# Four image blocks on one core: an involution's start, its passage to a convolution, and a Fourier gate's end, re-staged

## The chip, the cores and the metric

The kernel runs on one core of a Trainium2 chip, as one program with one launch. Its time is the device time in microseconds; three runs of the kernel before give 1874.28, 1877.03 and 1877.57 us, median 1877.03. Lower is better. The profile comes from one further execution of 1874.37 us, whose recorded span is 1872.6 us.

## The reference

The input is x, 4 images of 256 channels and 56 x 56 pixels, in float32. Four residual layers follow each other, each on the group norm of its input (32 groups of 8 channels, `_gn`):

```python
x = x + L0(_gn(x))   # involution: 7x7 taps computed per pixel, one tap set per 16 channels
x = x + L1(_gn(x))   # two 3x3 convolutions, 256 to 256 channels, with batch norms and ReLU
x = x + L2(_gn(x))   # involution again, with batch norms and ReLU
x = x + L3(_gn(x))   # Fourier gates:
    cf = sigmoid((real part of fft2(x), mean over pixels) @ W.T + b)     # one per channel
    sf = real part of fft2(mean of x over the channels)                  # one per pixel
    out = x * cf + x * sf
```

The mean of a two-dimensional transform over all its frequencies is the pixel at the origin, so cf needs only the first pixel of each channel (`first_of`). sf needs the channel mean and two small products with cosine and sine matrices.

An involution multiplies the normed input by a 64-row weight (`red`), giving 64 numbers per pixel, and these by `span`, giving 16 x 49 taps per pixel. Each tap multiplies the pixel at its offset, and the 49 results are added.

## The kernel before

**Blocks and units.** An image is two blocks of 128 channels (`cb` 0 and 1); a block is a tile of 128 x 3136 (1.6 MB) from a pool of three buffers (`new_block`). Eight units (image, block) run through the first involution, twelve row chunks through the convolutions, eight units through the second involution, and the gates of layer 3 run inside the second involution, an image behind. The results between the layers lie in DRAM (`src`).

**A unit of an involution** has two stages. In the first, `tap_matrices` (L471 to L489), 32 steps each make six products of the 64-row image `hp` (which lies in both halves of the partitions) with a table `z_sb`, three from each half. The result is copied out of PSUM with the bias table `zb_sb` added, by VectorE (L489) in three steps of four and by ScalarE (L482) in the fourth. In the second stage, `apply` (L513 to L540), seven columns of 8 pixels each multiply the taps `kt` by the windows `xw`. A column's windows are made three columns ahead: `next_strip` (L362, L364) norms a strip, `next_windows` transposes it (L381), copies it (L382) and shuffles it with four DMAs of `xw` into itself (L388, L390), 0.76 MB in all, issued by SP and in layer 0 partly by GpSimd.

**Work between.** Steps of other work are generators that are advanced at numbered steps of the first stage (`hooks`, steps 0 to 31) or after columns of the second (`late`): the sums of the next image (`sums`), the group norm (`norm_steps`: aggregate, product with `gavg_sb`, three VectorE steps, product, power on GpSimd, shift), the next image's 64 rows (`bottleneck`, L404 to L441), its loads. After `since = mark()`, `in_order(since)` binds each engine to the order in which the program was written; instructions before it are placed by a scheduler.

**Start of layer 0.** Both blocks of image 0 are loaded on SP in four pieces each. The norms of both are made, then `bottleneck(0)`: weights scaled by the norm (`redn`, L404), products for 9 image rows at a time in two halves of 64 output rows (L433), copied on ScalarE (L450) and across the halves by VectorE (L441). `make_tables` loads `span` on ScalarE's queue, copies it into `z_sb` (16 copies on VectorE, L300; two of biases, L308), makes the bias table by 24 products (L315) and copies it (L322). `batch_norms` follows. The same tables for layer 2 are made in unit 0, at steps 3, 14 and 21, and stored to DRAM on SP (L747, L748); the load of image 1 stands at step 23.

**Passage to the convolutions.** After the first column of unit 7, `begin_conv` issues on SP the first rows (L889) and both halves of the raw weights (L897, 1.18 MB each); the shuffles of the columns behind it stand after these on SP. The norm of the last block (L197 to L212) runs after the last column. The convolution begins with `row_weights` (loads L952, L953 on ScalarE's queue; six steps L964 to L966 on VectorE), `phases` (four on ScalarE, L1039, four on VectorE, L1037), `transform` (L1047 to L1069), and the first products (L1160).

**End of layer 3.** For the last image nothing else runs beside. After the norm, `channel_mean` scales a column of ones by the norm (L585), multiplies it with the block, 448 pixels at a time (L593, L596), adds the shift (L604), and turns the row of means into 56 x 56 by a store to DRAM and a load back (L607, L608). `gate_factors` loads the weights of cf (L616), makes cf (L623, L630), the first Fourier product (L639) and its copy `half` (L649). `last_gates` computes, for each of seven chunks of 8 image rows, the second Fourier product as eight products of 56 columns, each with one row of `half` spread over 128 columns as its weights (L700). Then per block: norm (L710), (sf + cf) times it (L713), add to the block (L715, block 0 on GpSimd, block 1 on VectorE), store (L716, GpSimd's and SP's queues).

## Time and profile before

| what | us |
|---|---|
| median of three runs | 1877.03 |
| profiled execution | 1874.37 |
| its span | 1872.6 |
| TensorE products busy | 1709.5 (91%) |
| weight loads busy | 1509.6 (81%) |
| VectorE busy | 1433.3 (77%) |
| ScalarE busy | 748.8 (40%) |
| GpSimd busy | 432.2 (23%) |
| first column product (L513) of unit 0 | starts at 74.02 |
| first convolution product (L1160) | starts at 548.45 |
| last GpSimd store (L716) | issued from 1864.57 |

A float32 product appears as two records in the trace, so "x48" of L315 is 24 products; a transpose is one. PE is the product, PEld its weight load. In the chain of waits each row has a start, a length and what ran or was waited for, followed back from the last instruction. In a table of windows the columns are the window, its length, the busy time of PE, PEld, VectorE, ScalarE and GpSimd with the number of instructions, the clock granted to TensorE as a share of full speed, the share of the 16 DMA engines and their rate.

### The profile page before, as it was taken

To read this page: it belongs to the slowest core of one execution; us is meant where nothing else is said; L and a number is where in the kernel's file an instruction comes from. 1 tells how busy PE (TensorE), PEld (TensorE's weight loads), DVE (VectorE), ACT (ScalarE), POOL (GpSimd) and SP (SyncE) were. 2 spreads that over 40 slices of the span, in tenths; PEclk is the share of its full clock that TensorE was granted. 3 is DMA by queue.
4 is the path that set the end of the run, shared out by engine and by line. 5 is a ranking of instruction groups with operands and counts; after the bars stand their busy time and mean duration, and the time that the engine had idled before them with its cause. 6 is when DMAs were issued, how large, how long until landed. Compare 5 with 4: busy or idle time off the path is not lost.

```text
span 1872.6 us, 55573 instructions
## 1 busy us (share of the span) xinstructions
PE 1709.5 (91%) x24030; PEld 1509.6 (81%) x24030; DVE 1433.3 (77%) x2823; ACT 748.8 (40%) x1657; POOL 432.2 (23%) x615
## 2 busy tenths in 40 slices
PE   5999999999759999999999999997999898898866
PEld 3888888888748988898899889885877777778865
DVE  5687777876678988898888988865767777777763
ACT  2445445454423222232223212114666565565532
POOL 2323433244210000000000000000000581681672
PEclk9999999999979999999999999998999999999995
DMA  3445544453533111110111210223533764773652
GB/s 97 150 146 177 153 120 140 152 153 111 160 121 100 42 60 61 61 67 36 62 58 57 73 35 33 89 76 89 174 107 132 231 193 147 222 215 105 177 147 76
DMA packets 65589, 215.72 MB, mean 115 GB/s; under 512 B 13564, under 2 KB 20528, under 8 KB 61504
## 3 DMA queue, kind: packets, MB, share of 16 engines
q1 hardware_dynamic: 44448, 141.62, 24.1%
q0 software_dynamic: 14848, 65.85, 10.9%
q10 hardware_dynamic: 6048, 4.68, 0.8%
q8 instruction: 190, 3.11, 0.7%
q14 instruction: 55, 0.45, 0.1%
HBM read 76.24 MB, written 49.16 MB: 67 GB/s over the span
## 4 chain that ended last, share of the span: by engine, by line
PE 65%; DVE 21%; DMA 5%; POOL 3%; issue 3%; ACT 2%; SPq 1%; POOLq 0%; ACTq 0%; DVEq 0%
PE mm L1242 20%; PE ps L513 14%; DVE kt L489 12%; PE mm L1160 10%; PE ps L471 7%; PE mm L1131 6%; PE ps L381 4%; DMA xw<-xw 3%; PE ps L433 2%; DVE un L533 2%; PE ps L700 1%; ACT hp L452 1%; PE ps L596 1%; DVE st L844 1%; DMA xs<-in_x_dram 1%
## 5 line engine op out<-in xcount | busy, mean ns | idle before, releaser
L513 PE MATMUL ps<-kt,xw 126*32 126x48 f32 (+1 forms) x12544 | 383.5, 236 | 56.9 <-DMA xw<-xw 21.3
L513 PEld LDWEIGHTS ps<-kt,xw 126*32 126x32 f32 (+1 forms) x12544 | 344.2, 122 | 102.4 <-issue 48.1
L471 PE MATMUL ps<-hp,z_sb 64*126 64x133 f32 x6144 | 389.0, 282 | 19.2 <-DVE kt L489 7.0
L471 PEld LDWEIGHTS ps<-hp,z_sb 64*126 64x126 f32 x6144 | 370.7, 189 | 34.1 <-DVE kt L489 8.7
L489 DVE TENSOR_TENSOR kt<-ps,zb_sb 126x798 f32<-126x798 f32 x384 | 357.9, 978 | 43.6 <-PE ps L471 43.1
L1242 PE MATMUL mm<-v,u_sb 128*128 128x280 f32 (+1 forms) x1728 | 384.9, 384 | 3.3 <-DVE v L1067 3.3
L1242 PEld LDWEIGHTS mm<-v,u_sb 128*128 128x128 f32 x1728 | 327.6, 190 | 57.8 <-DVE v L1067 3.6
L482 ACT ACTIVATE kt<-ps,zb_sb 126x133 f32<-126x133 f32 x768 | 224.0, 441 | 179.4 <-PE ps L471 179.4
L1160 PE MATMUL mm<-v,u_sb 128*128 128x252 f32 (+1 forms) x936 | 211.2, 386 | 12.6 <-DVE v L1051 12.6
L1160 PEld LDWEIGHTS mm<-v,u_sb 128*128 128x128 f32 x936 | 177.2, 190 | 42.9 <-issue 12.6
L533 DVE SCALAR_TENSOR_TENSOR un<-ps,par_sb,un 128x240 f32<-128x240 f32 x224 | 98.4, 457 | 103.1 <-ACT un L526 98.8
L533 DVE SCALAR_TENSOR_TENSOR un<-ps,s,un 128x240 f32<-128x240 f32 x224 | 102.3, 457 | 92.9 <-ACT un L528 88.7
L1279 POOL DMA_DIRECT2D x<-xs x24 | 13.1, 546 | 684.9 <-DVE xs L1278 539.5
L1227 ACT ACTIVATE res<-xs,shift,norm_sb 128x1120 f32<-128x1120 f32 (+1 forms) x24 | 30.2, 1260 | 235.2 <-DVE xs L1278 119.7
L538 POOL TENSOR_TENSOR xs<-un,xs 128x240 f32<-128x240 f32 x112 | 72.4, 665 | 224.2 <-DVE un L533 224.1
L382 ACT COPY xw<-ps 126x896 f32<-126x896 f32 x112 | 101.5, 907 | 49.6 <-PE ps L381 39.2
L381 PE MATMUL ps<-ident_sb,strip_sb 128*126 128x128 f32 x784 | 111.4, 282 | 1.6 <-DVE kt L489 0.8
L526 ACT ACTIVATE un<-ps,par_sb 128x240 f32<-128x240 f32 x112 | 50.1, 448 | 138.6 <-PE ps L513 136.7
L1131 PE MATMUL mm<-xs,u_sb 128*128 128x126 f32 (+1 forms) x792 | 98.3, 277 | 1.3 <-DVE xs L1094 1.0
L528 ACT ACTIVATE un<-ps,bn_t,s 128x240 f32<-128x240 f32 x112 | 60.1, 538 | 97.8 <-PE ps L513 93.7
L139 POOL TENSOR_TENSOR norm_sb<-norm_sb,mhalf 128x1 f32<-128x1 f32 x32 | 19.2, 602 | 341.7 <-DVE norm_sb L138 341.7
L1131 PEld LDWEIGHTS mm<-xs,u_sb 128*128 128x128 f32 x792 | 94.3, 191 | 2.7 <-issue 1.4
(194 smaller groups left out, 1973.0 us busy)
## 6 DMA issues: line engine op xcount, KB each, us to landing
xw<-xw SPq DMA_DIRECT2D x168, 252.0 KB
xw<-xw SPq DMA_DIRECT2D x224, 126.0 KB
xw<-xw POOLq DMA_DIRECT2D x56, 252.0 KB, 4.7
xs<-x SPq DMA_DIRECT2D x24, 560.0 KB
x<-xs POOLq DMA_DIRECT2D x8, 1568.0 KB, 7.9
xs<-x SPq DMA_DIRECT2D x8, 1568.0 KB
xs<-in_x_dram SPq DMA_DIRECT2D x6, 1568.0 KB
x<-xs SPq DMA_DIRECT2D x6, 1568.0 KB
```

The costliest lines, as they stand in the source:

```text
L381: nc.tensor.transpose(ps[:Q, k * P : (k + 1) * P], flat[:, k * Q : (k + 1) * Q], ident_sb)
L382: nc.scalar.copy(xw[:, :NSB, :], ps[:Q, : NSB * P].rearrange("q (n c) -> q n c", n=NSB))
L471: nc.tensor.matmul(ps[:Q, i, k * NT : (k + 1) * NT], z_sb[i * R : (i + 1) * R, cb * GB // 2 + gp, z0 : z0 + Q], hp[i * R : (i + 1) * R, py ...
L482: nc.scalar.activation(kt[:, g0 + i, pb, :, k], ps[:Q, i, k * NT : (k + 1) * NT], AF.Identity, bias=zb_sb[:, cb * GB + g0 + i, p0 + k : p0 ...
L489: nc.vector.tensor_tensor(kt[:, g0 : g0 + 2, pb], ps[:Q, :, : PB * NT].rearrange("q i (k t) -> q i t k", k=PB), zb_sb[:, cb * GB + g0 : cb ...
L513: nc.tensor.matmul(v[m * j : m * j + m, i, :, k * TP : (k + 1) * TP], xw[:, window(ty), m * j : m * j + m], kt[:, ng * j : ng * j + ng, :, ...
L528: nc.scalar.activation(part, o[0], AF.Identity, bias=bn["t4"][:, cb : cb + 1], scale=bn["s4"][ng][:, 0, cb : cb + 1])
L533: nc.vector.scalar_tensor_tensor(part, o[e], s, part, ALU.mult, ALU.add)
L538: nc.gpsimd.tensor_tensor(dst, u, dst, ALU.add)
L1131: nc.tensor.matmul(ps[:, co * m : (co + 1) * m], u[ci][:, co * P : (co + 1) * P], v2[:, e, : n // 2, ci * WT : (ci + 1) * WT], start=(ci = ...
L1160: nc.tensor.matmul(ps, u1_sb[:, ci, dy, k, co * P : (co + 1) * P], v[:, k, dy * NB + ci : (dy + n - 1) * NB + ci + 1 : NB, :], start=(j == 0),
L1242: nc.tensor.matmul(ps, u2_sb[:, ci, dy, k, co * P : (co + 1) * P], v[:, k, dy * NB + ci : (dy + n - 1) * NB + ci + 1 : NB, :], start=(j == 0),
```

## The change

- **Start (`begin`, `warm`, `load_block`).** Block 0 is loaded in two pieces, block 1 in four. `span`, biases and `red` are loaded on GpSimd's queue. ScalarE does a first small copy at once, and the 16 + 2 + 1 table copies. The products of block 0 with all 128 output rows (both halves alike) stand in TensorE's order before block 1's norm, in seven banks, and block 1's are added to them afterwards; the copies alternate between ScalarE and VectorE, without copies across the halves. TensorE gets 8, 2 and 8 products that nobody reads. All of this lies inside the written order. `batch_norms` is a generator, spread over the start and unit 0.
- **Unit 0.** The layer 2 tables are no longer made there; image 1's load moves from step 23 to step 16.
- **Last image of layer 0.** The layer 2 tables are made there: loads at step 16 of unit 6, the copies three at a time after its columns on ScalarE, the bias table in six pieces (after a column of unit 6 and at steps 3, 6, 10, 14 and 18 of unit 7), the stores at step 22.
- **Passage.** Rows and the second half of the raw weights are loaded at step 28 of unit 7 on SP, the first half in three parts after columns 0, 1 and 2 on ScalarE's queue. `row_weights` loads its two slices on SP. All eight `phases` of chunk 0 run on ScalarE. 28 products that nobody reads stand before the first of the convolution. The last block's norm is made inside the first convolution steps.
- **End.** Block 0's normed values are made ahead (`last_normed`); block 1's mean is made by group sums of the raw block: 56 products, one an image column, each with 56 weights columns and 16 moving ones, scaled by the norm afterwards and added on VectorE (`last_mean`). cf's weights are loaded at step 20 of the last unit. The second Fourier product is one 56 x 56 product, spread on VectorE into 8 rows a partition (`rows`, masked by `last_xn[0]`), and seven products of 448 columns. Block 1 is finished on ScalarE.

```diff
@@ start
-            for cb in range(NB):
-                if (0, cb) not in xs_of:
-                    load(0, cb, 3)
+            since = mark()
+            if layer == 0:
+                load(0, 0, (4, 3))
+                load(0, 1, (2, 2, 2, 1))
+
+                nc.scalar.copy(norm_sb[:, 3, B - 1, 1, :], mhalf)
...
-            def make_tables(z_sb, zb_sb, span, sb, scratch, eng):
+            def make_tables(z_sb, zb_sb, span, sb, scratch, eng, parts):
...
-                            nc.vector.tensor_copy(
+                            nc.scalar.copy(
                                 field(z_sb[half, cb * m + gp, :]),
                                 taps[half, cb, :, 2 * gp + i].rearrange("p (y x) -> p y x", x=KK),
                             )
+                            yield
...
+            def begin():
...
+                steps(tables, 17)
+                warm(8, xs_of[0, 0][:, :P])
+                steps(sums0, NCHUNK)
+                norm = norm_of(0, 0, 0, sums_of[0, 0])
+                steps(norm, 2)
+                next(folds)
+                steps(norm, 1)
+                warm(2, ident_sb)
+                steps(norm, 1)
+                steps(folds, 2)
+                steps(norm, 1)
+                steps(sums1, 2)
+                steps(norm, 1)
+                nc.vector.tensor_scalar_mul(redn[:, 0], red_sb[:, 0], rstd[:, 0:1])
+                steps(sums1, NCHUNK - 2)
+                next(tables)
+                warm(8, ident_sb)
...
+                for j in range(NH):
+                    products(j, 0)
+                steps(norm, 2)
...
+                for j in range(NH):
+                    products(j, 1)
...
@@ last image of layer 0
+                if last_image and cb == 0:
+                    g2 = tables2()
+                    place(hooks, g2, (16,))
+                elif last_image:
+                    place(hooks, g2, (3, 6, 10, 14, 18, 22, 23))
+                    hooks.setdefault(28, []).append(ahead[0])
...
+                if last_image and cb == 0:
+                    for tx in range(6):
+                        late[tx] += [step(g2)] * 3
+                elif last_image:
+                    for tx in range(3):
+                        late[tx].append(ahead[1 + tx])
...
@@ end
+            def last_mean(b, bank):
...
+                for x in range(W):
+                    nc.tensor.matmul(means[:, x // m, x % m, :], xs[:, x, :], by, start=True, stop=True)
+                yield
...
+                nc.vector.tensor_tensor(
+                    parts,
+                    means,
+                    scales[:, :ng].unsqueeze(1).unsqueeze(1).to_broadcast([H, 2, m, ng]),
+                    ALU.mult,
+                )
...
-                    for r in range(CR):
-                        y = j * CR + r
-                        nc.tensor.matmul(
-                            sf[:, r * W : (r + 1) * W],
-                            half[:, y : y + 1].to_broadcast([P, P]),
-                            cs2_sb,
-                            start=True,
-                            stop=True,
-                        )
+                    nc.tensor.matmul(sf, last_xn[1][:H, j : j + 1].to_broadcast([H, P]), rows, start=True, stop=True)
                     for cb in range(NB):
...
+                        if cb == 0:
+                            nc.gpsimd.tensor_tensor(xs, xs, xn, ALU.add)
+                            nc.gpsimd.dma_start(ov[b, cb][:, at], xs)
+                        else:
+                            nc.scalar.activation(xs, xn, AF.Identity, bias=back)
+                            nc.sync.dma_start(ov[b, cb][:, at], xs)
...
-            run(norm_of(layer + 1, b, cb, st))
...
@@ passage
     def begin_conv():
-        room["h"] = new_h()
-        room["rows"] = new_block()
         room["v2"] = new_block()
         load_rows(0, src[1])
-        for ci, t in enumerate((room["h"], room["v2"])):
-            nc.sync.dma_start(
-                t[:, : 9 * C], wc1[ci * P : (ci + 1) * P].rearrange("c k n -> c (k n)")
-            )
+        raw_weights(1, 0, 1, nc.sync)
+
+    def begin_weights(part):
+        if part == 0:
+            room["h"] = new_h()
+        raw_weights(0, part, 3, nc.scalar)
...
-                    nc.scalar.dma_start(u[:, ci, :, 0, :], w[:, :, 0, :])
-                    nc.scalar.dma_start(u[:, ci, :, 5, :], w[:, :, 2, :])
+                    nc.sync.dma_start(u[:, ci, :, 0, :], w[:, :, 0, :])
+                    nc.sync.dma_start(u[:, ci, :, 5, :], w[:, :, 2, :])
...
-            g = phases(0, nc.vector)
-            for _ in range(4):
-                next(g)
+            ps = one_bank()
+            for _ in range(28):
+                nc.tensor.matmul(ps[:, :P], ident_sb, ident_sb, start=True, stop=True)
             for _ in range(NB):
                 next(weights1)
-            run(g)
+            run(phases(0))
...
-            tail1, tail2, slow = [], [], []
+            tail1, tail2, slow = [], [], [norm_steps(st, one_bank, 1, B - 1, NB - 1)]
```

## The prediction

> **What bounds the kernel now.** I read the page first (TensorE busy 91% of the span, by far the busiest), then the chain of waits in order of time, then the stretches in which TensorE idles, as 4 us windows. The repeated units are bound by TensorE or VectorE and the change leaves their body alone; what it touches is three seams: the start, the passage from the first involution to the convolutions, and the end.
>
> The start, in the chain (start us, length us, what):
>
> ```profile
> 23.73 7.20 PE ps L433 x26
> 30.93 3.03 PE ps L315 x48
> 36.57 4.01 PE ps L471 x36
> 41.49 3.62 PE ps L471 x60
> ...
> 53.08 1.26 DVE xs L300 x8
> ...
> 57.17 3.95 PE ps L471 x36
> 61.12 2.74 PE ps L315 x48
> 63.86 8.10 PE ps L471 x108
> ...
> 74.02 3.22 PE ps L513 x97
> ```
>
> The first tap matrices begin at 36.57, after products (L433) and bias tables (L315). 36 of their records take 4.01 us there, 60 take 3.62 us at 41.49: the first run at half clock. At 53.08 VectorE copies the tables of the *second* involution, and at 61.12 TensorE makes them; the records around run at half clock again. So unit 0's tap stage lasts 37.5 us; that of unit 7 lasts 489.34 - 463.98 = 25.4.
>
> The passage:
>
> ```profile
> 497.56 3.25 PE ps L513 x103
> ...
> 502.57 16.40 DMA xw<-xw
> ...
> 519.11 10.28 PE ps L513 x251
> ...
> 543.05 2.81 DVE ph L1037 x4
> ...
> 548.45 30.35 PE mm L1160 x120
> ```
>
> The window shuffle (xw<-xw) of the fifth column, 0.76 MB a column, waits in the DMA rings behind 3.5 MB of convolution loads issued after the first column (L889, L897). The DMA share in that time is 0.86 to 1.06. Then 18.0 us pass between the last product (530.44) and the first of the convolution.
>
> The end, and its clock (columns of the second fence: window, length, busy PE, PEld, DVE, ACT, POOL, granted clock, DMA):
>
> ```profile
> 1826.31 3.05 PE ps L596 x14
> 1829.39 1.16 ACT xs L604 x2
> ...
> 1830.67 1.79 DMA m<-xs
> ...
> 1832.89 2.15 DMA xs<-in_w_dram
> ...
> 1838.16 20.71 PE ps L700 x96
> ```
>
> ```profile
> 1838.00:1842.00 4.00, 3.84 (x18) 3.87 (x19) 0.12 (x2) 1.35 (x3) 0.00 (x0) 0.50 0.00 0
> ```
>
> 24.1 us go to 56 products of 56 columns, at half clock; the weight loads are as busy as the products.
>
> **What the skill says.** "TensorE: Matmul & The Clock Gate", Part 1: the array runs at half clock until a window of about 3.4 us was busy, and falls back after an idle one. The trace agrees: in 1 us windows the clock changes at 33.4, 40.0, 57.1, 60.6, 64.0 and 67.4, all near multiples of 3.41 us apart. It adds something: the tables (16 columns a product) count as idle, since the window that holds them ends at half clock (64.0), and the 56-column products never warm it. The same page, "LDWEIGHTS": its time goes with the columns, not the rows. Here a 128-column load costs 24.0/112 = 0.214 us cold, twice the page's 128/1.2 GHz[...]. "DMA: Bandwidth & Descriptors", "Issuing engines are not separate DMA queues": all queues share 16 engines. The stall at 502.57 shows it, so a move between queues alone frees no bandwidth.
>
> **Start and unit 0.** I rebuild the time line. Same bytes as before, so block 0 is in at about 9.6 (before 9.36). VectorE sums its last three chunks to 11.4 (3 x 0.6), aggregate 0.34; TensorE 0.6; small steps 0.8; two warm products 0.85 (2 x 128 columns at half clock); TensorE 0.6: 14.0. The table copies on ScalarE (18, at an estimated 0.22 each from the 0.26 of one-column activations, L630) end before that. In TensorE's order now follow 48 table records, cold: 126-column loads in two row halves, 0.105 us each (the pace at 36.57, 4.01/36, is 0.11): 5.0, to 19.0. Eight warm products, cold, 0.43 each (two passes of 0.214): 22.4. The clock then rises. Block 0's seven products are 3136 columns of full width; L1242 shows 33.96 us for 72 products of 280 columns (144 records in the chain), 1.69 ns a column at full clock, so 5.3, and 0.3 for what runs cold: 28.0. (The old ones, two halves of 64 output rows side by side, take 0.42 us a product warm.) Here is the price of the new order: block 1's group sums (ready at 19.3, five chunks after the weight scaling at 16.1) are queued behind these. From 28.0: two products, small VectorE steps, the power on GpSimd (0.56), shift, weights: 3.1. Second products 5.3, last copies 0.7: first tap product at 37.1, warm. Removed from that path: six half copies (0.43 each) and their waits. Bounds: 33 if the tables run warm, 40 if block 0's products run cold.
>
> Unit 0's tap stage: 25.4 as unit 7, plus three window transposes (0.91 each): 28.1. First column product at 65.2, before 74.0: **gain 8.8**. The moved load of image 1 (step 16 instead of 23) stands behind nine shuffles whose sources are done by then: nothing.
>
> **Last image, tables of the second involution.** 48 table records warm are 2.8 us (2.74 at 61.12), cut in six. The 16 copies go to ScalarE, 40% busy, so free in unit 6's columns; their loads on SP wait for a store that lands 7.9 us after its issue at the unit's start, and stand half a tap stage later. In unit 7's tap stage TensorE had 384 records x 0.0603 = 23.2 us plus 0.76 for the norm, and VectorE 24 x 0.98 plus sums, so most of the 2.8 shows: **loss 2.5** (0.5 to 5 if PSUM rotation stutters).
>
> **Unit 7's columns.** Before 530.4 - 489.3 = 41.1 us. Without the stall: four columns at 4.13 (505.74 - 489.34 = 16.40) and three without transposes at 3.25: 26.2. What is late next: rows and half the weights (2.4 MB) are now issued at tap step 28, when the DMA share was 0.00 to 0.01 (475 to 493), about 8 us at 300 GB/s (279 and 334 GB/s in the windows from 4 to 12 us), so done near the first shuffle. The other half goes in three parts of 0.39 MB on ScalarE's queue beside three shuffles of 0.76 MB: 1.15 MB per 4.13 us is 278 GB/s, just under what the stall's windows moved. I allow 1.5 us. **Gain 13.4** (0 to 15).
>
> **Passage.** After the last product: copies, sums, GpSimd's adds 3.0 as before; scales 0.3; six weight steps at 0.96: 5.8; zeroing 0.2; three transform steps 2.4; 0.2: 11.9 against 18.0. Beside it ScalarE's eight phases (0.84 each, 6.7); before, ScalarE could not start until it had issued four loads (533.98 to 538.68), which SP now issues. They may end 1 us after VectorE is ready. The norm is off the path; its two products go into the convolution. **Gain 5** (2 to 6). The 28 warm products (0.21 each, 6 us) end about 5 us before the convolution starts, so they save the cold start (4 us at half clock, 2 us lost) only about half the time: **gain 1**.
>
> **End.** Last product before at 1818.4. Block 0's seven activations (0.69 each) follow on ScalarE, beside the rest. TensorE runs 56 mean products, 112 records with 56-column loads: 47 ns warm or 93 cold by the column rule, 5.2 to 10.4; strided loads appear nowhere in the trace, so I take 5.9 (mostly warm) and keep 12 as the far end; no reason allows less than 5. So 1824.3. Norm 3.0 (1822.17 to 1825.27 before); then VectorE: first, scales 0.5, 896-element multiply out of PSUM 1.0 (L489 moves 798 in 0.98), reduce 1.0, rest 0.5: 1830.3. DFT products 0.6 and 0.35, copies 0.44, row spread 0.6 (448 elements; L713 takes 0.64), first 448-column product 1.5 cold, multiply 0.65, handovers 0.5: first GpSimd add at 1835. Removed: row means, both m transfers and the w3 load of the path (now half a unit earlier). The loop: TensorE 1.5, VectorE 1.3, ScalarE 0.7, GpSimd 1.12 + 0.30 + 0.58 with its DMA = 2.05 a chunk (1842.66 to 1844.66). So **GpSimd is the new bound**: 6 x 2.05 + 2.0 after 1835 is 1849.2, before 1865.1 (0.56 after 1864.57). **Gain 15.9** (9 to 18).
>
> **Sum.** 8.8 - 2.5 + 13.4 + 5 + 1 + 15.9 = 41.6. Against the profiled execution, 1874.4 (span 1872.6): 1832.8. The median of the runs is 0.14% above that execution, so 1835.
>
> **Rivals.** *The shuffle stall stays*, moved to an earlier column, because the same bytes pass the same 16 engines: the columns' 13.4 go, 1848. For it: shares near 1 in the stall. Against: idle engines from 475 to 493. 0.12. *TensorE stays cold at both ends*: products of block 0 cold (+3) and strided, cold means (+6): 1844. For: tables count as idle. 0.13. *Slower*: SP is held in unit 6. The span loads at tap step 16 wait for a block's store; SP issues in order, and every later shuffle stands behind them. Half a tap stage and three ready windows cover about 25 us; beyond that each us counts, and from about 70 us of hold the sum turns. A 75 us hold gives 1885 with the start gained. Against: the longest such hold on SP (L240 for x<-xs) was 7.7 us. 0.04. *Nothing gained* is excluded unless stalls cancel: 0.02. The forecast itself, 1825 to 1843, has 0.69.
>
> **How the numbers follow.** The range reaches to the first rival and to a start with warm tables and an unhindered passage: 1820 to 1851. About 0.2% is what a measurement of this kernel can tell from no change. Faster 0.94, same 0.02, slower 0.04.
>
> **What would show it.** First tap product near 37 and warm, first column near 65; no xw wait over 2 us in unit 7; 12 to 13 us from the last involution product to the convolution; mean products 5 to 7 us; 2.05 us a chunk in the last loop with GpSimd never waiting. A first tap product after 41, a shuffle wait over 8 us, or a last loop slower than 3 us a chunk would make it wrong.

## The result, and the profile after

The changed kernel takes 1868.04 us (median of 7 runs, 1863.11 to 1871.42), the kernel before 1875.15 us (7 runs, 1874.28 to 1880.96): ratio 0.9957, interval [0.9939, 0.9975]. It is faster, by a sixth of the forecast 42 us in the medians and by a quarter in the profiles, and the time lies outside the stated range of 1820 to 1851 us. The profiled execution after is the fastest of its seven, 1863.11 us with a span of 1861.3, against 1872.6 before. So the two profiles differ by 11.3 us, and these can be laid out by stage. Each row is the difference of two distances between the same two events (in brackets: where the stage ends, before and after):

| stage, from and to | predicted gain | gain in the profiles |
|---|---|---|
| start and unit 0, to the first column product (74.02; 79.69) | 8.8 | -5.7 |
| units 0 to 5, to unit 6's first column (432.19; 437.65) | 0 | 0.2 |
| tables in units 6 and 7, to unit 7's first column (489.34; 500.95) | -2.5 | -6.1 |
| unit 7's columns (to 530.44; 531.45) | 13.4 | 10.6 |
| passage, to the first convolution product (548.45; 543.38) | 5 | 6.1 |
| convolutions, to layer 2's first tap product (1287.9; 1282.6) | 1 | 0.2 |
| layer 2, to its last product (1818.4; 1816.2) | 0 | -3.1 |
| the end (to 1872.6; 1861.3) | 15.9 | 9.1 |
| sum | 41.6 | 11.3 |

**The start.** The chain of waits of the changed kernel (start, length, what) now begins with a load of 1.2 KB:

```profile
2.26 11.58 DMA rp<-in_rpar_dram
...
14.09 3.71 DVE st L358 x7
...
52.52 2.32 PE ps L577 x36
```

VectorE's sums of block 0 (st, L358) start at 14.0, although the block's first chunk was there by 6.5. VectorE takes its instructions in the order written, and ahead of the sums stand four additions of the batch-norm folding (L138) that read the parameters cp and rp. These small loads landed at 12.3 and 13.8, beside six loads of x that kept the DMA engines at a share of 1.03 to 1.07 from 4 to 12 us. The first tap product (L577) comes at 52.52 instead of 36.57 before, warm as forecast; unit 0's tap stage then takes 27.2 us.

The second hole lies just ahead of that product. In the timeline (start, length, engine, line, operation, and in brackets the idle time before and its releaser) of the second products:

```profile
40.91 0.41 ACT L561 ACTIVATE hp<-ps,hb 128x168 f32<-128x168 f32 x1 [14.32 <-PE ps L527]
41.35 0.39 DVE L563 TENSOR_SCALAR hp<-ps,hb 128x168 f32<-128x168 f32 x1 [2.53 <-ACT hp L561]
41.77 0.40 ACT L561 ACTIVATE hp<-ps,hb 128x168 f32<-128x168 f32 x1 [0.46 <-DVE hp L563]
42.23 3.37 PE L527 MATMUL ps<-xs,redn 128*128 128x504 f32 x4 [1.36 <-ACT hp L561]
```

ScalarE and VectorE take turns: 11 of the 20 copies wait for the copy before them on the other engine. Only twice do two copies run at the same time (from 48.98 and 52.30), and these read different PSUM tiles. A tile here is two banks and holds two blocks of rows; the product of the second block waits for ScalarE's last copy of the first (the last line), although that lies in the other bank. From the start of the second products (38.82) to the first tap product pass 13.7 us; the products were costed at 5.3. Five of their 14 records run at half clock, at 0.84 us instead of 0.42.

**The passage.** TensorE's wait of 12.1 us on the shuffle (within the 16.40 us of DMA in the chain of before) is gone, and two smaller stalls are left in the middle of columns, which the profile puts down to nothing it shows ("issue"):

```profile
512.21 1.99 issue
...
522.92 1.66 issue
...
543.38 30.24 PE mm L1367 x120
```

From the last product (531.45) to the first convolution product pass 11.9 us. The convolution's first stage takes 30.24 us, 30.35 before: it still starts at half clock (granted clock 0.50 from 544 to 546, 1.00 from 547; before, 0.50 from 549 to 552).

**The end.** The 20.71 us of L700 are now 10.80 us of L889 in the chain. Ahead of it stand the mean products; the first line is from the chain, the second from the timeline, and the other two are 1 us windows (window, length, busy PE, PEld, DVE, ACT, POOL with numbers of instructions, granted clock, DMA):

```profile
1836.49 10.80 PE ps L889 x14
```

```profile
1816.17 11.75 PE L841 MATMUL ps<-gavg_sb,xs 128*56 128x16 f32 x112
```

```profile
1818.00:1819.00 1.00, 1.00 (x12) 1.00 (x11) 0.96 (x4) 1.00 (x3) 0.00 (x0) 1.00 0.01 4
1823.00:1824.00 1.00, 1.00 (x12) 1.00 (x12) 0.00 (x0) 0.00 (x0) 0.00 (x0) 0.50 0.00 0
```

The 112 records take 11.75 us, and they run at the same pace at full and at half clock: 12 records touch either window, and their starts lie 0.103 us apart in both. In the last loop GpSimd adds every 2.02 us without a wait (forecast 2.05); its first addition comes at 1839.18.

### The profile page after: what moved, and what is told of

Same layout as the page of the kernel before. It is cut to its first block, busy times and chain, and to the rows that moved or that the text cites. A ratio compares the mean times of both kernels' runs of the same rounds, so it can differ in the third digit from the quotient of the medians.

```text
span 1861.3 us, 55767 instructions
## 1 busy us (share of the span) xinstructions
PE 1723.9 (93%) x24120; PEld 1514.0 (81%) x24120; DVE 1415.0 (76%) x2786; ACT 763.1 (41%) x1700; POOL 439.2 (24%) x623
## 4 chain that ended last, share of the span: by engine, by line
PE 68%; DVE 18%; issue 4%; DMA 3%; ACT 3%; POOL 2%; SPq 1%; ACTq 0%; DVEq 0%; POOLq 0%
PE mm L1449 20%; PE ps L619 15%; PE mm L1367 10%; PE ps L577 10%; DVE kt L595 9%; PE mm L1338 5%; PE ps L407 4%; PE ps L459 2%; DVE un L639 1%; DMA xw<-xw 1%; ACT kt L588 1%; ACT hp L478 1%; DMA rp<-in_rpar_dram 1%; PE ps L889 1%; PE ps L702 1%
## 5 line engine op out<-in xcount | busy, mean ns | idle before, releaser
L577 PE MATMUL ps<-hp,z_sb 64*126 64x133 f32 x6144 | 385.5, 280 | 17.2 <-issue 4.5
L577 PEld LDWEIGHTS ps<-hp,z_sb 64*126 64x126 f32 x6144 | 366.4, 187 | 32.4 <-issue 7.9
L1367 PEld LDWEIGHTS mm<-v,u_sb 128*128 128x128 f32 x936 | 177.1, 190 | 34.4 <-issue 4.2
L407 PEld LDWEIGHTS ps<-ident_sb,strip_sb 128*126 128x126 f32 x784 | 84.3, 141 | 19.0 <-issue 9.1
```

The costliest lines, as they stand in the source:

```text
L407: nc.tensor.transpose(ps[:Q, k * P : (k + 1) * P], flat[:, k * Q : (k + 1) * Q], ident_sb)
L577: nc.tensor.matmul(ps[:Q, i, k * NT : (k + 1) * NT], z_sb[i * R : (i + 1) * R, cb * GB // 2 + gp, z0 : z0 + Q], hp[i * R : (i + 1) * R, py ...
L1367: nc.tensor.matmul(ps, u1_sb[:, ci, dy, k, co * P : (co + 1) * P], v[:, k, dy * NB + ci : (dy + n - 1) * NB + ci + 1 : NB, :], start=(j == 0),
```

## Experiments on the start

Ratios are to the kernel before, run beside each; the changed kernel's is 0.9957. Stage times come from one profile per kernel.

**The folding moved behind the sums.** Its first step (L138) becomes its third, which is reached behind block 1's sums.

```diff
-            rsqrt_eps(bn["s" + name], par(var), BN_EPS)
-        yield
...
+        for name, par, _, _, _, var, n in folds:
+            rsqrt_eps(bn["s" + name], par(var), BN_EPS)
+        yield
         for i in range(3):
...
-                next(folds)
                 steps(tables, 17)
...
```

> The changed kernel with one move in the order of the start: the first step of the batch-norm folding (four additions on VectorE that read the parameter loads cp and rp, and their powers on GpSimd) no longer stands ahead of block 0's sums but among the small steps of block 1's norm. Nothing else differs. Theory: VectorE's order is served strictly, so the sums of block 0, whose first chunk is there at 6.5 us, wait in the changed kernel until rp lands at 13.8; with the move they begin near 6.5 to 8, end near 11.5 to 12, block 0's shift follows near 13, and everything behind it comes 4 to 6 us earlier: first tap product at 47 to 48.5 instead of 52.5, kernel 0.9957 - 0.0026 = about 0.993 of the time before. Rival: the start is bound by something else on the way (the tables' loads or copies, the clock, the loads of block 1), then the sums move but the first tap product stays within 1.5 us of 52.5 and the time stays where it is.

Ratio 0.9921 [0.9906, 0.9936]. The sums began at 5.98 and ended at 11.4, block 0's weights were scaled at 15.2, and the first tap product came at 46.1: 6.4 us earlier. The theory holds, the rival falls. From here the old working fits well: block 0's products run from 22.6 (forecast 22.4) to 29.2 (28.0), second products start at 32.45 (31.1).

**Products first, copies by row.**

```diff
                 for j in range(NH):
                     products(j, 1)
+                for j in range(NH):
...
+                        m = (TX, 0, TX // 2)[py]
+                        if m > 0:
+                            nc.scalar.activation(dst[:, :m], part[:, :m], AF.Identity, bias=hb)
+                        if m < TX:
+                            nc.vector.tensor_scalar_add(dst[:, m:], part[:, m:], hb)
```

> The changed kernel with another order of the start's last stage: all seven second products are issued before the first copy, and the copies are dealt out by row (row 0 on ScalarE, row 1 on VectorE, row 2 half and half) so that the two engines never write the same row's stretch. Nothing else differs. Theory: the 12.8 us of the second products (5.3 to 6.7 would be their own time) come from copies that wait for each other across the engines and from products of odd blocks that wait for the copies of the even one in the same two-bank tile; without both, the products take 6 to 7 us and the copies end about 1 us after the last, the first tap product comes at 45 to 46.5 instead of 52.5, and the kernel gains 6 to 7 us, 0.992 of the time before. Rival: the copies themselves are the limit (20 of 0.4 us each with their hand-overs on two engines, and the half clock of TensorE beside them); then less than 2.5 us are gained.

Ratio 0.9942 [0.9922, 0.9963]. The products no longer waited for copies, but the copies went on in turns from 42.1 to 50.6 (timeline; 20 of 26 wait for the other engine), and 12.3 us passed to the first tap product:

```profile
38.38 8.46 PE L527 MATMUL ps<-xs,redn 128*128 128x504 f32 x14 [0.18 <-DVE redn L542]
43.71 0.41 ACT L563 ACTIVATE hp<-ps,hb 128x168 f32<-128x168 f32 x1 [0.37 <-DVE hp L565]
44.15 0.39 DVE L565 TENSOR_SCALAR hp<-ps,hb 128x168 f32<-128x168 f32 x1 [0.47 <-ACT hp L563]
```

Seven of the 14 product records ran at half clock here (0.84 us instead of 0.42), so the first copy came 3.8 us after their start, in the next run after 2.0: by this estimate 1.8 of the 12.3 us are the clock's. By its number the rival won. Its reason was tested next.

**Copies by PSUM tile.**

```diff
-                        if (j + py) % 2 == 0:
+                        if j // 2 % 2 == 0:
```

> The changed kernel with the second products of the start issued before the copies, as in the run before, but the 20 copies dealt out by PSUM tile (the blocks of tiles 0 and 2 on ScalarE, of 1 and 3 on VectorE) instead of by row. Theory: the two engines took turns in the run before because they read the same PSUM tile, which the program's dependences serialize whatever they write; with a tile to each engine none of the copies waits for the other engine, they go on beside the products, and from the start of the second products to the first tap product pass 7.5 to 9 us instead of 12.3 to 13.7; the start gains 4.5 to 5.5 us on the changed kernel. Rival: the copies waited for each other through the tile that they write (hp), then dealing them by tile changes nothing and 12 us remain.

Ratio 0.9914 [0.9881, 0.9948]. 6.7 us instead of 12.3 passed (37.65 to 44.36): products 5.35, last copies 1.29. The first copies of each tile wait for products alone:

```profile
39.65 1.86 ACT L562 ACTIVATE hp<-ps,hb 128x168 f32<-128x168 f32 x6 [13.31 <-PE ps L527]
41.34 2.36 DVE L564 TENSOR_SCALAR hp<-ps,hb 128x168 f32<-128x168 f32 x8 [3.69 <-PE ps L527]
43.03 1.87 ACT L562 ACTIVATE hp<-ps,hb 128x168 f32<-128x168 f32 x6 [1.51 <-PE ps L527]
```

All products ran at full clock in this run, so the two runs differ by the clock as well; the waits do not depend on it. None of the 20 copies waits for the other engine, here and in the four later kernels with this edit, which take 6.7 us each, all at full clock. In the ten profiles with the changed kernel's copies 11 or 12 of the 20 wait, 5 to 12 of the 14 product records run at half clock, and 13.7 to 16.8 us pass. So the copies took turns because both engines read one PSUM tile, not because of what they wrote: they still write one tile. The Trainium skill, "PSUM — Partial Sum Buffer", "PSUM bank collisions raise a hardware error", says that the compiler back end adds a dependency between any two instructions on different engines that touch the same bank and 32-partition quadrant, "reads and writes alike". The traces agree for copies out of one bank. They also show a wait that a rule by bank does not ask for, the product at 42.23 above that waits for a copy out of the tile's other bank; so that wait at least goes by the program's tile. Whether the back end or the kernel's own framework placed the others was not separated.

**All of the start.** Folding and copies as above, and block 1's norm products ahead of block 0's seven, with three warm products after each in place of the eight before:

```diff
                 next(tables)
-                warm(8, ident_sb)
...
+                steps(norm, 2)
+                warm_bank(3)
+                steps(norm, 2)
+                warm_bank(3)
                 for j in range(NH):
                     products(j, 0)
-                steps(norm, 2)
-                next(folds)
-                steps(norm, 2)
-                next(folds)
                 steps(norm, 2)
```

> The changed kernel with three edits at the start only: the batch-norm folding later (as in the first experiment), block 1's norm products ahead of block 0's seven products on TensorE with three warm products after each (in place of the eight before), and the second products issued ahead of copies dealt out by PSUM tile. Theory: the prediction's time line for the start was wrong in three places only (sums behind rp, copies in turns, and the norm behind the products, which it had priced at 3.1 us): tables end at 19.0, block 0's products run 22.5 to 29.2, second products to 35.5, first tap product at 36.5 to 39 instead of 52.5; the kernel gains 13 to 16 us, about 0.988 of the time before. Rival: the start is bound by TensorE's own work at half clock or by late loads of block 1; then the first tap product stays after 43.

Ratio 0.9858 [0.9832, 0.9883], 1852.07 us. The chain shows the second products, the last copies and the first tap product:

```profile
30.92 5.19 PE ps L525 x12
36.14 1.29 ACT hp L566 x4
37.43 0.04 issue
37.47 2.32 PE ps L582 x36
```

First tap product at 37.47 (the prediction said 37.1), first column product at 64.98 (65.2). The forecast start can be reached; the changed kernel's order misses it. It took an order that the prediction did not have: of the norm's 3.3 us behind block 0's products 1.4 are left (29.48 to 30.92). That third edit was not run alone.

## Experiments on the last image and the passage

**The tables in one piece.**

```diff
-                yield from make_tables(z2, zb2, span2, sb2, scratch, nc.sync, 6)
+                yield from make_tables(z2, zb2, span2, sb2, scratch, nc.sync, 1)
...
-                    place(hooks, g2, (3, 6, 10, 14, 18, 22, 23))
+                    place(hooks, g2, (18, 22))
...
-                        late[tx] += [step(g2)] * 3
+                        late[tx] += [step(g2)] * (3 if tx < 5 else 2)
```

> The changed kernel with the bias tables of the second involution made in one piece of 24 products (48 records) at step 18 of unit 7's tap stage instead of six pieces of four, one of them in unit 6's sixth column. The work is the same. Theory: of the 6.2 us that the last image lost up to its first column product, 2.8 are the products and the rest are hand-overs, once a piece: a PSUM tile of the rotation that is held for 4 small products, and ScalarE's copy of it in between the tap activations; in one piece 3.0 to 4.0 us are lost. Rival: each table product costs what it did, wherever it stands, and the single copy of 384 columns (1.1 us on ScalarE) holds the tap stage as long; then 5.5 us or more stay lost.

Ratio 0.9937 [0.9918, 0.9956]. From the first column product of unit 6 to that of unit 7 pass 57.2 and 56.5 us in two profiles before, 63.3 and 64.3 in two of the changed kernel, 58.7 here, with all 48 records in one stretch of 2.74 us:

```profile
486.04 2.74 PE ps L340 x48
```

The other profiles agree: 61.6 to 63.8 us in the ten others with six pieces, 58.1 to 60.4 in the three others with one. So one piece loses 1 to 4 us on the kernel before, about the 2.74 us of the work, and six pieces lose 5 to 8. The changed kernel's chain holds 3.0 us of its pieces, and ahead of the first, in unit 6's columns, TensorE waits 1.6 us for ScalarE's copy of the bias fields. The rest of the 6.1 us is not assigned: 1.5 us in the transposes behind the first piece have no releaser, but such waits make 1.9 us in this stretch before and 2.4 after. As the run changes the number of pieces and the place of the first together, the two were not separated.

**The weights late.**

```diff
                     for tx in range(3):
-                        late[tx].append(ahead[1 + tx])
+                        late[4 + tx].append(ahead[1 + tx])
```

> The changed kernel with the three loads of 0.39 MB of convolution weights that ScalarE issues in unit 7's columns moved from columns 1 to 3 to columns 5 to 7, behind the last window shuffle. Nothing else differs. Theory: the two stalls of 2.0 and 1.7 us in unit 7's columns (in the middle of columns 3 and 5, not at their start) come from these loads on the shared DMA engines; without them the seven columns take 26.2 to 27.5 us instead of 30.5, the weights are in before the convolution's weight steps need them, and the kernel gains 2.5 to 4 us. Rival 1: the stalls come from the rows and the first half of the weights issued in the tap stage, or from the shuffles themselves; then 30 us remain. Rival 2: the late loads hold up the passage, which then takes 3 us longer than 11.9, and nothing is gained.

Ratio 0.9943 [0.9922, 0.9964]. The two stalls shrank from 2.0 and 1.7 us to 0.2 and 0.3; the columns took 28.35 us (501.64 to 529.99) instead of 30.50, the passage 11.9 as in the changed kernel. One profile would not carry this: in the changed kernel's second one a single stall of 2.2 us is left, and the columns take 29.2 us. Over all profiles they take 29.2 to 34.0 us with the loads early (twelve) and 28.4 to 29.5 with the loads late (four). The theory holds for the place of the loads; the gain, 2.1 us here, is under what was expected and too small for the times to show.

## Experiments on the end

**The norm between the means.** Its two products follow the 25th and the 41st mean product instead of the last:

```diff
                 for x in range(W):
                     nc.tensor.matmul(means[:, x // m, x % m, :], xs[:, x, :], by, start=True, stop=True)
+                    if x in (24, 40):
+                        yield
...
```

> The changed kernel with another order at the end: the last norm's two small products stand between the 56 mean products on TensorE (after the 25th and the 41st) instead of behind them. Nothing else differs. Theory: the norm's small steps, 3.0 us from the end of the means to its end, are then covered by the mean products, and the last loop begins about 3 us earlier (first addition on GpSimd at 1836 on the changed kernel's time base instead of 1839.2); the kernel gains 2.5 to 3 us. Rival: what follows the means is held by ScalarE, which still makes the normalized chunks, or by the products that need the norm; then under 1 us is gained.

Ratio 0.9928 [0.9902, 0.9955]. From the start of the means to GpSimd's first addition pass 21.2 us instead of 23.0: 1.8 gained. The norm's steps are covered, but its two products keep their 0.52 us each on TensorE.

**The mean by rows.**

```diff
-                xs = xs_of[b, cb].rearrange("p (h w) -> p w h", w=W)
+                xs = xs_of[b, cb].rearrange("p (h w) -> p h w", w=W)
...
+                nc.tensor.transpose(bank[:W, 32 : 32 + H], m2_of[0], ident_sb[:H, :H])
...
-                nc.tensor.matmul(ps[:H, :W], half, cs2_sb, start=True, stop=True)
+                nc.tensor.matmul(ps[:H, :W], cs2_sb, half, start=True, stop=True)
```

> The changed kernel with the mean of the last block taken by rows instead of by columns of the image: each of the 56 mean products loads 56 neighbouring elements of a partition instead of 56 that lie 56 apart; so the mean comes out turned, the other half's mean is turned by one more product, and the DFT's second product swaps its operands. Theory A (the strided load sets the pace, whatever the clock): the 112 records fall from 11.75 us to 5.2 (all at full clock, 47 ns a record, half of the 93 that 56 columns would take cold) to 7.5 us, and the kernel gains 4 to 6 us. Theory B (the clock sets it, 93 ns cold): the means stay at 10 us or more and under 1.5 us is gained.

Ratio 0.9948 [0.9929, 0.9967]. The means took 10.05 us, nearly all at half clock (TensorE idled 1.8 us ahead of them, waiting on ScalarE). Two windows lie to either side of the clock's fall:

```profile
1824.00:1824.60 0.60, 0.60 (x13) 0.60 (x13) 0.57 (x3) 0.60 (x2) 0.45 (x1) 1.00 0.00 0
1826.00:1827.00 1.00, 1.00 (x13) 1.00 (x13) 0.03 (x1) 1.00 (x2) 0.00 (x0) 0.50 0.06 16
```

The starts of the first records lie 0.052 us apart, those of the rest 0.093. So loads of neighbouring elements follow the clock, and the strided ones above do not: 0.103 us at either. Theory B's number came because the clock was half, yet A is right on the strided loads. Neighbouring elements save 10% at half clock and half at full clock, but a whole stage of these products was never at full clock: in both kernels it fell within 4 us of their start and stayed at half.

**The means by column.** Eight products behind each column of the last unit, copied to SBUF by ScalarE; eight remain at the end.

```diff
+                if last and layer == 2:
+                    for tx in range(1, NTX):
+                        late[tx].append(lambda tx=tx: mean_column(b, tx - 1))
...
```

> The changed kernel with 48 of the 56 mean products of the end taken earlier: the eight of a column of the last unit are issued behind the next column's products, and ScalarE copies their 128 results a column to SBUF; only the eight of the last column stay behind the last product, ahead of the norm. The work is the same but for these copies. Theory: the mean's 11.75 us (56 strided loads at one pace whatever the clock) stand alone on the path at the end, while TensorE idles some 7 us in the last unit's 36 us of columns; so the end gains about 8 us (from the last product to the first addition on GpSimd 14 to 16 us instead of 23.0), the last unit's columns lose 3 to 7 of the 10 us that move into them, and the kernel gains 2 to 6 us. Rival: the columns of the last unit are bound by TensorE itself, so that the whole 10 us appear there and nothing is gained, or the products wait for the additions of their column on VectorE and more is lost.

Ratio 0.9935 [0.9916, 0.9954]. From the last product to the first addition pass 15.3 us instead of 23.0, so 7.7 are gained there; the last unit's columns take 39.7 us, 34.2 and 35.6 in the changed kernel's profiles. Over all profiles these columns take 33.2 to 37.5 us without this edit (twelve) and 36.6 to 39.7 with it (four), so they give back some 3 us. The median lies lower by 0.2%, but the intervals overlap: the gain at the end is shown by the traces, the net gain not by the times.

**Everything mended.** Start reordered, tables in one piece, weights late, means by column.

> The four mended seams together on the changed kernel: the start reordered, the weights' loads late in unit 7's columns, the tables in one piece in its tap stage, the means of the last unit by column. Theory: the four gains lie at different places of the chain and add up: 15 to 16 us at the start, 2 in unit 7's columns, 3 to 5 in the tables, 2 to 6 at the end: 22 to 29 us under the changed kernel, 0.980 to 0.984 of the time before; with that the prediction's 1835 us is reached or nearly reached. Rival: the later layers take part of it back, since an earlier start only meets the same DMA waits later; then under 18 us are gained.

Ratio 0.9819 [0.9802, 0.9837], 1842.82 us: 1.4% under the changed kernel's ratio, some 26 us. The sum theory holds.

## Experiments on layer 2, which the change leaves alone

Two stages of the same instructions and bytes need not take the same time. A second profile of each kernel:

> The kernel before, unchanged, for a second profile of it. In its first profile layer 2 (from the first tap product of unit 8 to the last product) took 530.5 us; in the changed kernel's 533.6, and in its variants 530.1 to 542.6. If the change slowed layer 2 down, this run shows 528 to 532 again; if these are the differences from run to run of one and the same stage, it shows something from 530 to 542.

> The changed kernel, unchanged, for a second profile of it: layer 2 from 530 to 542 us if it differs from run to run, 533 to 535 if it does not; the first tap product again at 52 to 56 us.

Layer 2 took 530.8 us (530.5) before and 534.4 (533.6) after; the first tap product came at 53.7 after. TensorE's waits by releaser differ in kind. The changed kernel in layer 2 (line, releaser, us in total, times, longest):

```profile
PE ps L619 <- issue: 7.3, 7, 1.7
PE ps L619 <- DMA xw<-xw: 5.8, 7, 1.9
PE ps L407 <- issue: 5.5, 4, 2.7
```

With 4.5 and 2.5 us at two more lines (L577, L459) its waits put down to nothing are 19.8 us; before, they are 11.3, all at the column products:

```profile
PE ps L513 <- issue: 11.3, 11, 2.2
```

The DMA part of the page has a queue of the kind "instruction", with 80 packets of 16 KB in this stage and 190 in the whole execution, in which TensorE has 48,792 instructions: one packet for 257 of them. In units 6 and 7 of layer 0 such a packet starts 0.6 to 1.1 us ahead of each of three such stalls. If these are fetches of instructions that come late behind data, it matters where a block of 256 instructions ends. By the compiled programs, and by a count in the traces, TensorE's is 190 instructions longer than before's where layer 2 begins. Warm products in the passage shift that place, and nothing else in layer 2:

```diff
-            for _ in range(28):
+            for _ in range(44):
```

The shortened one has 12 in the same line, the mended ones 47 and 15.

> The changed kernel with 44 instead of 28 warm products in the passage to the convolutions. TensorE's program is by 190 instructions of 64 bytes longer than before's where layer 2 begins; the 16 products add 64, and so layer 2's instructions lie again as before's do against blocks of 256 instructions (16 KB), two instructions off. Nothing in layer 2 is changed. Theory: layer 2's waits with no releaser are fetches of such blocks that come late behind data, and which of them hurt depends on where a block ends; with before's place layer 2 takes 530 to 532 us again and these waits fall from 19 to 24 us to 11 to 14. Rival: they differ by chance; then layer 2 takes 533 to 543 us as in the other variants. Beside this the warm products end near 542.7 instead of 539.4, so the first stage of the convolution may lose its cold start (30.2 us there, of which up to 2 could go).

> The changed kernel with 12 instead of 28 warm products in the passage: TensorE's program is 126 instructions longer than before's where layer 2 begins, half a block of 256 away from before's place. Theory: another place, another sum of waits; layer 2 need not be at 533 to 543 us, and its waits stand at other lines than in the changed kernel. Rival: the place means nothing; layer 2 as in the changed kernel, 533 to 538 us, with the same waits. The convolution's first stage stays cold as in the changed kernel (30.2 us).

> The four mended seams together, and 19 warm products more in the passage, which put layer 2's instructions where before's are against the blocks of 256. Theory: layer 2 falls from 535.4 us to 530 to 533, and the kernel gains 2 to 5 us on the run without them, 0.979 to 0.981 of the time before. Rival: no difference (0.982).

> The four mended seams together, with 15 instead of 28 warm products in the passage; TensorE's program is then 126 instructions longer than before's where layer 2 begins, as in the shortened changed kernel. Theory: the waits without releaser in layer 2 go with the place of the blocks: they fall from 17 us in the mended kernel to 5 to 9, all at the same kinds of line as in the shortened one; layer 2 takes 528 to 532 us instead of 535 and the kernel gains 3 to 6 us on the mended one, 0.979 of the time before, though the convolution's first stage stays cold. Rival: chance; the waits are at 11 to 20 us again, and layer 2 at 533 to 540.

| place, instructions past before's | waits without releaser in layer 2, us | waits on DMA, us | layer 2, us |
|---|---|---|---|
| 0 (before, twice) | 11.3, 13.7 | 10.9, 11.2 | 530.5, 530.8 |
| 254, two short of a block (padded; mended and padded) | 11.0, 13.9 | 10.7, 10.8 | 527.9, 536.1 |
| 178 to 190 (changed kernel twice, its ten variants without other warm products) | 17.1 to 23.9 | 3.5 to 7.8 | 530.1 to 543.7 |
| 126 (shortened; mended and shortened) | 5.8, 10.0 | 15.3, 7.2 | 530.0, 532.5 |

The shortened kernel's waits of this kind are at the column products again:

```profile
PE ps L619 <- issue: 5.4, 6, 2.1
```

The ratios are 0.9929 [0.9904, 0.9954] padded, 0.9903 [0.9879, 0.9927] shortened, 0.9826 [0.9800, 0.9851] mended and padded, and 0.9812 [0.9790, 0.9835] mended and shortened, the fastest, 1838.73 us. The waits go with the place: none of 18 profiles breaks the order. A count ties them to the blocks. With TensorE's instructions numbered from the start of each trace, all 246 waits without a releaser in layer 2, in all 18 profiles, end at an instruction whose number modulo 256 is 193 or 194; of 620 waits over 0.4 us that have a releaser, 7 do. And the 217 over 0.4 us without one end 1.2 to 1.9 us after a packet of the instruction queue has landed. So these stalls are at the fetch of the next block, by place and by time. Why a few of a stage's 80 fetches come late and most do not is not shown; that data ahead of them holds them up is argued, from the weights moved in unit 7.

Layer 2's time follows less surely: where these waits are short, those on DMA are mostly longer (why was not tested), and the mended and padded kernel still took 536.1 us, one stall of 4.9 us among its waits. The gains that were expected of the two mended variants are not seen: their intervals overlap with the mended kernel's. The shortened kernel's interval lies below the changed one's, by some 0.5% in the medians; its one profile (span 1862.1 us) is no shorter than the changed kernel's (1861.3), so the traces don't show where that time went.

## Why the prediction was wrong, step by step

- **"VectorE sums its last three chunks to 11.4"** failed. The estimate followed block 0's bytes and not the order of VectorE, in which cp and rp are read first. With that order mended the sums end at 11.4. (The terms listed after them add up to 14.6 and not to 14.0; with the order mended the step ends at 13.9, as some of them overlap.)
- **"Second products 5.3, last copies 0.7"** failed: 13.7 us. The products that had their copies beside them were costed by TensorE alone and at full clock; the copies out of one tile took turns, products waited for them, and five records ran at half clock. With a PSUM tile to each engine 6.7 us are measured. These two steps, 6.4 us by the first experiment and 7.0 by the copies by tile (the clock included), are 13.4 of the 14.5 us missed at the start. The steps between, and the price of the norm behind block 0's products (3.1; measured 35.49 to 38.82, 3.3), were right.
- **Tables, loss 2.5**: that the products show was right, the size not: 6.1, beyond the far end of 5. The products were priced by their time in one piece, which loses 1 to 4 us; six pieces, the first of them where it waits 1.6 us for ScalarE, lose 5 to 8. Waits for PSUM hardly show (0.3 us on ScalarE's copies, 0.2 before).
- **Unit 7's columns, 27.7**: 30.5. The shuffle stall went, as forecast; 4.3 us stood over the stall-free 26.2 where 1.5 were allowed, and 2.1 of them went when the weights were moved. They were stalls with no releaser, at the borders of instruction blocks, not waits on the shuffle.
- **Passage, gain 5**: right; 11.9 us as worked out, without the 1 us allowed for ScalarE. **Clock, gain 1**: not seen; the warm products end 4.0 us ahead of the convolution. Where they ran up to it (both padded kernels), its first stage took 34.4 us for the same 144 records; in the changed, mended and shortened ones it took 35.9 to 36.8.
- **Mean products, "I take 5.9 (mostly warm) and keep 12 as the far end"**: the wrong end was taken. 11.75 us account for 5.85 of the 6.8 us missing at the end. The rule by columns and clock holds for neighbouring elements (0.052 and 0.093 us measured by rows, 0.047 and 0.093 forecast); loads with this stride take 0.103 at either clock, which no line of the profile of before could show.
- **Layer 2 at nothing**: 3.1 lost in the profiles. A longer program ahead of it moved the borders of its instruction blocks, and the waits there grew from 11.3 to 19.8 us; the time of the stage scatters from 527.9 to 543.7 us over all kernels, so the 3.1 themselves are not assigned.
- **The rivals.** "TensorE cold at both ends" came nearest for the end by its number, not by its reason, as the pace was the same warm; at the start it was the second products that ran cold in part. The shuffle stall did not stay, and no product of units 6 and 7 waited for a shuffle, so SP was not held long enough to matter.

The common fault, strided loads and layer 2 apart: each new stage was costed by its busiest engine, with the order of the other engines' instructions and their shared buffers taken as free.

## What to carry to other kernels

When an order is written out by hand, walk through every engine's list up to its first wait, small parameter loads included: one wait for 1.2 KB at its head holds all that follows. Two engines that read the same PSUM tile worked in turns here, so try dealing work out by tile. Work that is cut into pieces has to be priced at the place where each piece stands, and a duration measured without a stride doesn't price a strided load. A wait without a releaser can be looked up by the number of its instruction.

## What the runs showed of the hardware

- Loading 56 elements that lie 56 apart as weights costs 0.103 us a record at granted clock 1.00 and 0.50 alike; 56 neighbouring ones cost 0.052 at 1.00 and 0.093 at 0.50.
- Loads of 13 and 1.2 KB, issued by 2.3 us, landed at 12.3 and 13.8 us beside large ones.
- The sum of TensorE's waits without a releaser in an unchanged stage ranged from 5.8 to 23.9 us with the length of the program ahead of it; all 246 such waits end at the same place in a block of 256 instructions, those over 0.4 us within 1.2 to 1.9 us of the landing of a 16 KB packet of instructions.
